# Graph attention on one core: scores with the summed node on the partitions, a fixed softmax shift, values in two column tiles

## The chip, the cores and the metric

One core of one Trainium2 chip. The metric is the device time of one execution in microseconds (us), the median of the runs shown. TensorE is called PE (PEld is its weight loading), VectorE DVE, ScalarE ACT, GpSimd POOL; SP issues DMAs.

## The reference, cut to what matters

x is [8, 2048, 64], adj a [2048, 2048] table of 0 and 1; all else is fp32. All products here are fp32.

```python
def _gat_layer(h, mask, b):                       # h: [..., N, 64]
    scores = einsum('...nd,...md->...nm', h, h)
    scores = where(mask, scores, -1e16)
    attn = softmax(scores, axis=-1)
    return einsum('...nm,...md->...nd', attn, h) + b
mask = adj + eye(N) > 0
h = einsum('bnc,hdc->bhnd', x, Wh)                # 4 heads
out_h = _gat_layer(h, mask, bh)
z = leaky_relu(concat of the heads, 0.2)
h2 = einsum('bnk,dk->bnd', z, Wo)
z2 = leaky_relu(_gat_layer(h2, mask, bo), 0.2)
out = layernorm(x + layernorm(z2) * gamma + beta)
```

The raw scores h h^T are symmetric, and so is nothing else: the mask isn't, and the softmax is taken over m, the summed node.

## The kernel before, in words

Feature maps go in pairs of 64 channels on the 128 partitions (two heads of one batch element in layer 1, two batch elements in layer 2). There are 20 such pairs, called units: 16 of the first layer and 4 of the second. A unit holds hT [128 = 2 x 64 channels, 2048 nodes], which is both operands of the scores, and hN [128 nodes, 16 blocks, A | 1 | B], the values with 64 columns of ones between the two maps.

A unit goes through its 2048 rows n in 8 groups of 256, so there are 160 groups. For a group:

- `scores` (L186): n stands on the partitions, m on the free axis. Map j uses the array's rows 64j to 64j+63, as its 64 channels lie on these partitions. One DVE pass (L192) takes a score tile of 128 x 1024 out of PSUM, adds the mask (0 or -1e16, bf16) and keeps the row's extreme; a small second instruction reads that accumulator. When a row is whole, ACT makes exp with the row's extreme as its bias (L197, 128 x 2048).
- `values` (L210, L213/L215, L226): the product with the values sums over m, so e must have m on the partitions. For each of 16 blocks of m, four 128 x 128 transposes on PE (L210) write one PSUM bank, ACT or DVE copies it out (L215, L213), and two products with hN (L226) take 256 moving columns each. The ones in hN make the denominators come out of the same products, spread over 64 partitions.
- Then DVE takes reciprocals of the denominators (L235, L236), multiplies, adds the bias, applies leaky ReLU (L237 to L241), and `project` (L249, L251) or, in layer 2, `finish` (the LayerNorms, L268 to L293) follows.

The scores of the next group are put between the products of the running one (`between`, called four times). The order on each engine is the scheduler's. POOL has little to do: at the start it turns 16 rows of adj into the mask (L136), and later one small power in each LayerNorm (L283).

A fp32 product shows in the trace as two MATMUL rows, each with its weight load; one such row is called a pass here. A transpose is one pass.

Of the kernel before, what the change touches and what calls it, by code (L numbers as in the profile page):

```python
"""GAT layer (4 heads, then one output layer) over a dense masked graph, leaky ReLU, LayerNorm,
residual, LayerNorm, on one core.

Feature maps are handled in pairs of 64 channels on the 128 partitions: two heads of one batch
element in the first layer, two batch elements in the second. For a pair the kernel holds
  hT [128 = 2 x 64 channels, N]      both operands of the scores
  hN [128 nodes, N / 128, A | 1 | B] the values; the ones give the softmax denominators, already
                                     spread over 64 partitions, in the product that weighs the values.
Rows go through in groups of 256: scores in fp32, the mask added as 0 / -1e16 and the row extreme
taken in one VectorE pass out of PSUM, exp on ScalarE, transposes and values on TensorE. The scores  # L10
of a group are issued between the products of the group before it.
"""
# [1 line left out]

# [6 lines left out]
F32 = mybir.dt.float32  # L21
I32 = mybir.dt.int32
BF16 = mybir.dt.bfloat16
AF = mybir.ActivationFunctionType
OP = mybir.AluOpType
AX = mybir.AxisListType

NEG = -1e16
EPS = 1e-5
SLOPE = 0.2  # L30
FMAX = 3.4028234663852886e38


@with_exitstack
def gat_kernel(ctx: ExitStack, tc: tile.TileContext, x, adj, Wh, bh, Wo, bo, gamma, beta, out):
    nc = tc.nc
    B, N, C = x.shape
    H, D, _ = Wh.shape
    P = 128
    NB = N // P          # blocks of 128 nodes  # L40
    GI = 2               # blocks in a group
    GR = GI * P
    NG = NB // GI
    HP = H // 2
# [7 lines left out]
    psum = ctx.enter_context(tc.tile_pool(name="psum", bufs=2, space=bass.MemoryType.PSUM))  # L52

    def slot(dtype, name):
        """One of the slots of N words that the scores and everything that is only passing share."""
        return epool.tile([P, N], dtype, tag="e", name=name)

    def bank(name):
# [2 lines left out]
    turn = [0]  # L61

    def evacuate(dst, src):
        """PSUM to SBUF, shared between ScalarE and VectorE."""
        turn[0] += 1
        if turn[0] % 2:
            nc.scalar.copy(dst, src)
        else:
            nc.vector.tensor_copy(dst, src)

# [1 line left out]
    ident = const.tile([P, P], F32, name="ident")  # L72
    make_identity(nc, ident)
    whT = const.tile([P, H * D], F32, name="whT")       # [channel (twice), (h d)]
    woT = const.tile([P, HP, D], F32, name="woT")       # [k in a pair of heads, pair, d]
    bh2 = const.tile([P, HP], F32, name="bh2")
    bo2 = const.tile([P, 1], F32, name="bo2")
    gam = const.tile([P, D], F32, name="gam")
# [45 lines left out]
    for t in hNs + [h2N]:  # L124
        nc.gpsimd.memset(t[:, :, 1, :], 1.0)

# [1 line left out]
    bias = {}  # L128

    def load_mask(r):  # L130
# [4 lines left out]
        bias[r] = const.tile([P, N], BF16, name=f"bias{r}")  # L135
        nc.gpsimd.tensor_scalar(bias[r], st, 0.0, NEG, OP.is_le, OP.mult)  # L136

# [1 line left out]
    class Unit:  # L139
        def __init__(self, n, bp, b2, hp):  # L140
            self.n, self.bp, self.b2, self.hp = n, bp, b2, hp
# [26 lines left out]
                    evacuate(self.hN[:, 4 * c:4 * c + 4, 2 * j, :], pv[:, :, j, :])  # L168

        def scores(self, g, step):  # L170
            """Half of the score rows of one block, for both maps; exp once a row is whole."""
            n = self.n
            i, half = divmod(step, 2)
            r = g * GI + i
            if half == 0:
                if r not in bias:
                    load_mask(r)
                for j in range(2):
                    self.E[g, i, j] = (slot(F32, f"e{n}_{g}_{i}_{j}"),
                                       small.tile([P, 2], F32, tag="mx", name=f"mx{n}_{g}_{i}_{j}"))  # L180
            ps = [psum.tile([P, HALF], F32, tag="s", name=f"s{n}_{g}_{step}_{j}") for j in range(2)]
            for c in range(HALF // 512):
                for j in range(2):
                    rows = slice(j * D, (j + 1) * D)
                    c0 = half * HALF + c * 512
                    nc.tensor.matmul(ps[j][:, c * 512:(c + 1) * 512], self.hT[rows, r * P:(r + 1) * P],  # L186
                                     self.hT[rows, c0:c0 + 512], start=True, stop=True)
            cols = slice(half * HALF, (half + 1) * HALF)
            for j in range(2):
                e, mx = self.E[g, i, j]  # L190
                # e = -(scores + bias); mx = its least so far, minus the row's maximum in the end
                nc.vector.tensor_tensor_reduce(  # L192
                    out=e[:, cols], in0=ps[j], in1=bias[r][:, cols], scale=-1.0,
                    scalar=mx[:, 0:1] if half else FMAX, op0=OP.add, op1=OP.min,
                    accum_out=mx[:, half:half + 1])
                if half:
                    nc.scalar.activation(e, e, AF.Exp, bias=mx[:, 1:2], scale=-1.0)  # L197

        def values(self, g, between):
            """The products with the values of a group, `between` called four times on the way.  # L200
            Returns what is left to do with their result."""
            n = self.n
            O = [psum.tile([P, GR], F32, tag=f"o{j}", name=f"o{n}_{g}_{j}", bufs=1) for j in range(2)]

            def turned(m):
                p = bank(f"pt{n}_{g}_{m}")
                for j in range(2):
                    for i in range(GI):
                        k = (j * GI + i) * P
                        nc.tensor.transpose(p[:, k:k + P], self.E[g, i, j][0][:, m * P:(m + 1) * P], ident)  # L210
                t = work.tile([P, 512], F32, tag="et", name=f"et{n}_{g}_{m}", bufs=2)
                if m % 8 in (1, 4, 7):
                    nc.vector.tensor_copy(t, p)  # L213
                else:
                    nc.scalar.copy(t, p)  # L215
                return t

            t = None
            for m in range(NB):
                if m % 4 == 0:  # L220
                    between(m // 4)
                if t is None:
                    t = turned(m)
                ahead = turned(m + 1) if m + 1 < NB else None
                for j in range(2):
                    nc.tensor.matmul(O[j], self.hN[:, m, j:j + 2, :].rearrange("p a d -> p (a d)"),  # L226
                                     t[:, j * GR:(j + 1) * GR], start=(m == 0), stop=(m == NB - 1))
                t = ahead
            for i in range(GI):
                for j in range(2):  # L230
                    del self.E[g, i, j]
            lo, hi = slice(0, D), slice(D, 2 * D)
            rz = work.tile([P, GR], F32, tag="rz", name=f"rz{n}_{g}")
            z = work.tile([P, GR], F32, tag="z", name=f"z{n}_{g}")
            nc.vector.reciprocal(rz[lo], O[0][hi])  # L235
            nc.vector.reciprocal(rz[hi], O[1][lo])  # L236
            nc.vector.tensor_mul(z[lo], O[0][lo], rz[lo])  # L237
            nc.vector.tensor_mul(z[hi], O[1][hi], rz[hi])
            b = bo2 if self.second else bh2[:, self.hp:self.hp + 1]
            nc.vector.tensor_scalar(z, z, b, None, OP.add)  # L240
            nc.vector.scalar_tensor_tensor(z, z, SLOPE, z, OP.mult, OP.max)  # L241
            return lambda: self.finish(g, z) if self.second else self.project(g, z)

        def project(self, g, z):
            """These heads' part of the second layer's feature maps, for the group's nodes."""
            p = bank(f"pp{self.n}_{g}")
            w = woT[:, self.hp, :]
            rows = slice(self.b2 * D, (self.b2 + 1) * D)
# [12 lines left out]
                nc.vector.tensor_add(hN, hN, pn)  # L261

        def finish(self, g, z):
            """LayerNorm, residual and LayerNorm of the group's nodes, in rows."""
            n, K = self.n, 2 * GI
            p = bank(f"pf{n}_{g}")
            for i in range(GI):
# [34 lines left out]
        units.append(Unit(len(units), bp, 0, None))  # L302

    todo = [(u, g) for u in units for g in range(NG)]
    started = False      # whether the scores of this group went out between the last one's products
    rest = None          # what is left of the last group
    xst = None
    for k, (u, g) in enumerate(todo):
        if not started:
            # The second layer needs every node of the first.  # L310
            if rest is not None:
                rest()
                rest = None
            if g == 0:
                u.prepare()
            for s in range(2 * GI):
                u.scores(g, s)
# [19 lines left out]
    rest()  # L337


# [1 line left out]
_INS = ["x", "adj", "L0_gnn_Wh", "L0_gnn_bh", "L0_gnn_Wo", "L0_gnn_bo", "L0_gnn_gamma", "L0_gnn_beta"]  # L341
_OUTS = [((8, 2048, 64), "float32")]
# [23 lines left out]
```

## Time and profile before

| | |
|---|---|
| Median of 3 runs | 6328.17 us (6324.19 to 6332.58) |
| Span of the profiled execution, first to last instruction | 6325.3 us |
| Busy shares of the span | PE 96%, PEld 60%, DVE 53%, ACT 34%, POOL 3% |
| Mean granted PE clock, as a share of 2.4 GHz | 0.981 |
| DMA over the span | 29.60 MB, mean 5 GB/s |

The span is the profiled execution's own time from its first to its last instruction. The median of the runs lies 2.9 us over it; that is what stands around it, launch and end, and chance. A timeline row gives start, duration, engine, line, operation, tiles, form and count of instructions merged. For PE the durations overlap: a MATMUL's row lasts beyond the start of the next, so what a pass takes in a stream is the distance from start to start.

### The profile page before, as it was taken

How to read it: one execution, taken by the hardware profiler on the slowest of the kernel's cores; microseconds unless marked ns; L12 is line 12 of the kernel's file. 1: busy time of each engine (PE TensorE's matmuls, PEld its weight loads, DVE VectorE, ACT ScalarE, POOL GpSimd, SP SyncE). 2: the span in 40 equal slices, each digit the busy share in tenths (PEclk: the TensorE clock that was granted, in tenths of full speed). 3: DMA queues.
4: the chain of work that ended last, by engine and by line, in shares of the span. 5: the costliest groups of instructions: out<-in, count | busy, mean ns of one | idle time of the engine just before them, and what ended most of it. 6: DMA issues, size and time to landing. Idle time of an engine off the chain costs nothing.

```text
span 6325.3 us, 65156 instructions
## 1 busy us (share of the span) xinstructions
PE 6055.8 (96%) x27204; PEld 3770.4 (60%) x27204; DVE 3348.6 (53%) x5402; ACT 2170.2 (34%) x2345; POOL 184.6 (3%) x95
## 2 busy tenths in 40 slices
PE   7899999999999999999999999999999999999998
PEld 4556666655566666665556666566555666666555
DVE  4445555556555555555655555555565555555555
ACT  2233333333333333333333333333333333333332
POOL 3210000000000000000000000000000000000000
PEclk9899999999999999999999999999999999999999
DMA  1100000000000000000000000000000000000000
GB/s 62 40 14 1 1 1 1 1 1 11 3 1 1 1 1 1 1 1 1 11 3 1 1 1 1 1 1 1 9 4 2 1 1 1 1 1 1 1 3 5
DMA packets 37303, 29.60 MB, mean 5 GB/s; under 512 B 34864, under 2 KB 34928, under 8 KB 34960
## 3 DMA queue, kind: packets, MB, share of 16 engines
q1 hardware_dynamic: 36224, 25.17, 1.4%
q8 instruction: 213, 3.49, 0.2%
q14 instruction: 82, 0.67, 0.0%
q10 hardware_dynamic: 624, 0.20, 0.0%
q0 software_dynamic: 160, 0.07, 0.0%
HBM read 21.24 MB, written 4.19 MB: 4 GB/s over the span
## 4 chain that ended last, share of the span: by engine, by line
PE 76%; ACT 12%; DVE 7%; POOL 2%; issue 2%; DMA 1%; ACTq 0%; POOLq 0%; SPq 0%; DVEq 0%
PE o L226 30%; PE s L186 26%; PE pt L210 16%; ACT e L197 9%; ACT et L215 2%; DVE e L192 2%; POOL bias L136 1%; PE pp L251 1%; PE pp L249 1%; POOL st L283 1%; PE pn L164 1%; PE ph L157 1%; DVE et L213 1%; DMA adj<-in_adj_dram 0%; DVE st L281 0%
## 5 line engine op out<-in xcount | busy, mean ns | idle before, releaser
L226 PE MATMUL o<-et,hN 128*128 128x256 f32 x8192 | 2160.0, 389 | 110.1 <-ACT et L215 84.3
L215 ACT COPY et<-pt 128x512 f32<-128x512 f32 x1600 | 931.4, 583 | 3677.4 <-PE pt L210 3190.2
L186 PE MATMUL s<-hT 64*128 64x512 f32 x4096 | 1766.0, 640 | 34.3 <-DVE mx L192 34.3
L226 PEld LDWEIGHTS o<-et,hN 128*128 128x128 f32 x8192 | 1422.9, 192 | 606.0 <-ACT et L215 280.3
L210 PEld LDWEIGHTS pt<-ident,e 128*128 128x128 f32 x10240 | 1211.0, 142 | 822.1 <-ACT et L215 256.0
L210 PE MATMUL pt<-ident,e 128*128 128x128 f32 x10240 | 1596.5, 279 | 25.2 <-DVE y L289 11.5
L213 DVE COPY et<-pt 128x512 f32<-128x512 f32 x960 | 661.5, 689 | 1463.7 <-PE pt L210 973.1
L197 ACT ACTIVATE e<-e,mx 128x2048 f32<-128x2048 f32 x640 | 1262.7, 2001 | 263.8 <-DVE mx L192 252.3
L192 DVE CUSTOM_DVE_ANT_0 e<-s,bias 128x1024 f32<-128x1024 f32 x640 | 772.0, 1223 | 732.0 <-PE s L186 634.0
L192 DVE CUSTOM_DVE_ANT_0 e<-s,bias,mx 128x1024 f32<-128x1024 f32 x640 | 806.5, 1281 | 394.4 <-PE s L186 394.4
L186 PEld LDWEIGHTS s<-hT 64*128 64x128 f32 x4096 | 529.6, 188 | 536.7 <-issue 450.6
L226 PE MATMUL o<-et,h2N 128*128 128x256 f32 x2048 | 545.5, 392 | 39.9 <-ACT et L215 21.9
L186 PE MATMUL s<-h2T 64*128 64x512 f32 x1024 | 453.8, 660 | 28.3 <-DVE mx L192 28.3
L226 PEld LDWEIGHTS o<-et,h2N 128*128 128x128 f32 x2048 | 357.2, 194 | 147.9 <-ACT et L215 52.6
L235 DVE RECIPROCAL rz<-o 64x256 f32<-64x256 f32 x160 | 281.4, 1759 | 191.3 <-PE o L226 191.2
L236 DVE RECIPROCAL rz<-o 64x256 f32<-64x256 f32 x160 | 280.1, 1751 | 5.1
L186 PEld LDWEIGHTS s<-h2T 64*128 64x128 f32 x1024 | 137.6, 193 | 172.0 <-issue 110.0
L283 POOL TENSOR_TENSOR st<-st,mhalf 128x4 f32<-128x4 f32 x64 | 64.5, 1007 | 5889.0 <-DVE st L282 5889.0
L136 POOL TENSOR_SCALAR bias<-adj 128x2048 bf16<-128x2048 int32 x16 | 113.6, 7097 | 246.9 <-DVE adj L134 246.9
L192 DVE DVE_READ_ACCUMULATOR2_ANT mx<- 128x1 f32 x1280 | 106.2, 83 | 0.0
L251 PEld LDWEIGHTS pp<-woT,z 128*128 128x128 f32 x512 | 69.6, 197 | 52.8 <-issue 52.8
L241 DVE SCALAR_TENSOR_TENSOR z<-z 128x256 f32<-128x256 f32 x160 | 88.0, 550 | 0.2
(60 smaller groups left out, 1100.1 us busy)
## 6 DMA issues: line engine op xcount, KB each, us to landing
adj<-in_adj_dram SPq DMA_DIRECT2D x16, 1024.0 KB, 6.8
x<-in_x_dram SPq DMA_DIRECT2D x8, 512.0 KB, 5.6
out_dram<-y SPq DMA_DIRECT2D x64, 64.0 KB, 1.7
ws<-in_L_gnn_Wh_dram ACTq DMA_DIRECT2D x2, 64.0 KB, 4.4
ws<-in_L_gnn_Wo_dram ACTq DMA_DIRECT2D x1, 64.0 KB, 4.6
bo<-in_L_gnn_bo_dram POOLq DMA_DIRECT2D x2, 0.2 KB, 5.5
gam<-in_L_gnn_gamma_dram POOLq DMA_DIRECT2D x1, 32.0 KB, 5.6
bet<-in_L_gnn_beta_dram POOLq DMA_DIRECT2D x1, 32.0 KB, 5.2
```

The costliest lines, as they stand in the source:

```text
L136: nc.gpsimd.tensor_scalar(bias[r], st, 0.0, NEG, OP.is_le, OP.mult)
L186: nc.tensor.matmul(ps[j][:, c * 512:(c + 1) * 512], self.hT[rows, r * P:(r + 1) * P], self.hT[rows, c0:c0 + 512], start=True, stop=True)
L192: nc.vector.tensor_tensor_reduce(out=e[:, cols], in0=ps[j], in1=bias[r][:, cols], scale=-1.0, scalar=mx[:, 0:1] if half else FMAX, op0=OP. ...
L197: nc.scalar.activation(e, e, AF.Exp, bias=mx[:, 1:2], scale=-1.0)
L210: nc.tensor.transpose(p[:, k:k + P], self.E[g, i, j][0][:, m * P:(m + 1) * P], ident)
L213: nc.vector.tensor_copy(t, p)
L215: nc.scalar.copy(t, p)
L226: nc.tensor.matmul(O[j], self.hN[:, m, j:j + 2, :].rearrange("p a d -> p (a d)"), t[:, j * GR:(j + 1) * GR], start=(m == 0), stop=(m == NB ...
L235: nc.vector.reciprocal(rz[lo], O[0][hi])
L236: nc.vector.reciprocal(rz[hi], O[1][lo])
L251: nc.tensor.matmul(p[:, GR + i * D:GR + (i + 1) * D], z[:, i * P:(i + 1) * P], w, start=True, stop=True)
L283: nc.gpsimd.tensor_tensor(st[:, 3, :], st[:, 2, :], mhalf, OP.pow)
```

## The change

The kernel becomes two programs behind each other. `fast_kernel` is new; `general_kernel` is the kernel before, unchanged, and runs only if a flag says so. The order on each engine in the new program is the order in which it is written (`manual_schedule`).

In `fast_kernel` the summed node m is on the partitions. Work goes in **periods**: 4 blocks m of 128 nodes against a chunk c of 512 rows n, for both maps of a unit. 4 periods make a chunk, 16 a unit, 320 all. In a period:

- `scores`: for each m, two products (map 0 on the array's rows 0 to 63, map 1 on 64 to 127) give 128 x 1024; DVE subtracts the mask (0 or 1e16, bf16, now stored transposed, one tile read for both maps); ACT takes exp with one constant shift per layer (78, and 62 in layer 2) in place of the row's extreme. A score tile takes two PSUM banks, and there are three of them.
- `values`: for each m of the period before, map j's 64 value columns are the weights, exp of map j is moving (512 columns), and the result goes to partitions 64j to 64j+63 of one bank. So each product uses 64 of the array's 128 columns. No transposes of e, no copies of them, no ones.
- `add_up`: the denominators. POOL adds three of four exp tiles (128 x 1024) into `acc`, DVE adds the fourth into `accd`.
- After a chunk, spread over the six next periods: `finish0` (ACT copies the result out of PSUM, DVE adds accd to acc), `finish1` (a product with ones sums acc over the partitions), `finish2` (the sums go by DMA to 128 partitions x 8, reciprocal, by DMA through DRAM and back, spread over 64 partitions), `finish3` (multiply, leaky ReLU), `finish4` (projection, or in layer 2 transposes and the first LayerNorm), `finish5` (layer 2: the rest).
- The biases are added to the values (bhb, bob), since the weights of a row sum to 1. hN is made by transposes of hT. The mask's 32 half rows are turned by PE transposes (bf16) at the start and during the first periods. Layer 2 of a pair of batch elements runs after the first unit of the next pair (the last two at the end), so that it need not wait for the projections of its own first layer.
- At the end the sums of all denominators and of their reciprocals on each partition are compared with e^83 and e^63, and a flag goes to DRAM. If one is over its limit, `general_kernel` computes everything again.

```diff
+        def scores(self, c, m):
+            ps = spsum(f"s{self.n}_{c}_{m}")
+            for j in range(2):
+                rows = slice(j * D, (j + 1) * D)
+                nc.tensor.matmul(ps[:, j * W:(j + 1) * W], self.hT[rows, m * P:(m + 1) * P],
+                                 self.hT[rows, c * W:(c + 1) * W], start=True, stop=True)
+            e = slot([P, 2, W], F32, f"e{self.n}_{c}_{m}")
+            nc.vector.tensor_tensor(e, ps.rearrange("p (j i) -> p j i", j=2),
+                                    mask[c][:, m, :].unsqueeze(1).to_broadcast([P, 2, W]), OP.subtract)
+            nc.scalar.activation(e, e, AF.Exp, bias=shifts[:, 1:2] if self.second else shifts[:, 0:1], scale=1.0)
+            return e
+
+        def values(self, c, m, e):
+            if m == 0:
+                self.O[c] = psum.tile([P, W], F32, tag="o", name=f"o{self.n}_{c}", bufs=1)
+            for j in range(2):
+                nc.tensor.matmul(self.O[c][j * D:(j + 1) * D, :], self.hN[:, m, j * D:(j + 1) * D], e[:, j, :],
+                                 start=(m == 0), stop=(m == NB - 1))
+
+        def add_up(self, c, es):
...
+            for e in es[:3]:
+                nc.gpsimd.tensor_tensor(self.acc[c], self.acc[c], e, OP.add)
...
+                nc.vector.tensor_tensor(t, t, es[3], OP.add)
...
+        def finish0(self, c):
+            self.osb[c] = wtile(f"osb{self.n}_{c}")
+            nc.scalar.copy(self.osb[c], self.O[c])
+            nc.vector.tensor_tensor(self.acc[c], self.acc[c], self.accd[c][0], OP.add)
+
+        def finish1(self, c):
...
+            for j in range(2):
+                nc.tensor.matmul(pz[j * D:(j + 1) * D, :], ones, self.acc[c][:, j, :], start=True, stop=True)
...
+        def finish3(self, c):
+            z = self.osb[c]
+            nc.vector.tensor_tensor(z, z, self.rz[c], OP.mult)
+            nc.vector.scalar_tensor_tensor(z, z, SLOPE, z, OP.mult, OP.max)
...
+    for t in range(total + 1):
+        now = []
+        if t < total:
+            u, c, q = periods[t]
+            now = [u.scores(c, q * BATCH + k) for k in range(BATCH)]
+        if t > 0:
+            u, c, q = periods[t - 1]
+            for k in range(BATCH):
+                u.values(c, q * BATCH + k, es[k])
+            u.add_up(c, es)
+        es = now
+        for job in jobs.pop(t, ()):
+            job()
...
+    nc.vector.tensor_scalar(fl, pf[0:1, 0:1], P - 0.5, None, OP.is_lt)
+    nc.sync.dma_start(out=flag, in_=fl)
+
+
+def gat_kernel(tc: tile.TileContext, x, adj, Wh, bh, Wo, bo, gamma, beta, out):
+    nc = tc.nc
+    with tc.tile_pool(name="flags", bufs=1, space=bass.MemoryType.DRAM) as pool:
+        flag = pool.tile([1, 1], I32, name="flag")
+        with tc.manual_schedule():
+            fast_kernel(tc, x, adj, Wh, bh, Wo, bo, gamma, beta, out, flag)
+        again = nc.values_load(flag, min_val=0, max_val=1)
+        with tc.If(again > 0):
+            general_kernel(tc, x, adj, Wh, bh, Wo, bo, gamma, beta, out)
```

On PE before, the middle of a group of the first layer. s are scores, pt transposes of e, et their copies, o the products with the values; the last numbers of a name tell tiles apart.

```order
L210 MATMUL pt_2_1_5744<-ident,e_2_1_0_5628 128x128
L210 MATMUL pt_2_1_5744<-ident,e_2_0_1_5523 128x128
L210 MATMUL pt_2_1_5744<-ident,e_2_1_1_5630 128x128
L186 MATMUL s_3_1_0_5780<-hT_5070 128x512
L210 MATMUL pt_2_2_5753<-ident,e_2_0_0_5521 128x128
L210 MATMUL pt_2_2_5753<-ident,e_2_1_0_5628 128x128
L210 MATMUL pt_2_2_5753<-ident,e_2_0_1_5523 128x128
L210 MATMUL pt_2_2_5753<-ident,e_2_1_1_5630 128x128
L186 MATMUL s_3_1_0_5780<-hT_5070 128x512
L226 MATMUL o_2_0_5723<-et_2_0_5742,hN_106 128x256
L226 MATMUL o_2_1_5724<-et_2_0_5742,hN_106 128x256
```

On PE in the new program, one period of the first layer (each x2 is map 0, then map 1), with the sum over the partitions of the chunk before (pz) behind it:

```order
L520 MATMUL s_0_4_5763<-hT_5437 128x512 x2
L520 MATMUL s_0_5_5769<-hT_5437 128x512 x2
L520 MATMUL s_0_6_5775<-hT_5437 128x512 x2
L520 MATMUL s_0_7_5781<-hT_5437 128x512 x2
L532 MATMUL o_0_5787<-e_0_0_5724,hN_5530 64x512 x2
L532 MATMUL o_0_5787<-e_0_1_5730,hN_5530 64x512 x2
L532 MATMUL o_0_5787<-e_0_2_5736,hN_5530 64x512 x2
L532 MATMUL o_0_5787<-e_0_3_5742,hN_5530 64x512 x2
L566 MATMUL pz_3_5799<-acc_3_5626,ones 64x512 x2
```

The transposes and the copies that they waited for have left the stream, and scores and values alternate in blocks of eight products, the values one period behind.

On DVE in the new program, a period that ends a chunk and the one after it. e are the subtractions of the mask, accd and acc the sums for the denominators, osb the result of the chunk before:

```order
L523 TENSOR_TENSOR e_3_15_10107<-s_3_15_10104,mask_124 128x1024
L553 TENSOR_TENSOR accd_3_10075<-accd_3_10075,e_3_11_10061 128x1024
L589 TENSOR_TENSOR osb_2_9993<-osb_2_9993,rz_2_10083 128x512
L590 SCALAR_TENSOR_TENSOR osb_2_9993<-osb_2_9993 128x512
L523 TENSOR_TENSOR e_0_0_10127<-s_0_0_10124,mask_121 128x1024
L523 TENSOR_TENSOR e_0_1_10133<-s_0_1_10130,mask_121 128x1024
L523 TENSOR_TENSOR e_0_2_10139<-s_0_2_10136,mask_121 128x1024
L523 TENSOR_TENSOR e_0_3_10145<-s_0_3_10142,mask_121 128x1024
L553 TENSOR_TENSOR accd_3_10075<-accd_3_10075,e_3_15_10107 128x1024
L560 TENSOR_TENSOR acc_3_10029<-acc_3_10029,accd_3_10075 128x1024
```

Every period's four subtractions stand in one block, and what a chunk leaves to do stands between two blocks, ahead of the next period's first subtraction.

## Rows read from the trace of the kernel before

**Rows 1.** The page: span, busy time by engine, granted clock in 40 slices.

```profile
span 6325.3 us, 65156 instructions
PE 6055.8 (96%) x27204; PEld 3770.4 (60%) x27204; DVE 3348.6 (53%) x5402; ACT 2170.2 (34%) x2345; POOL 184.6 (3%) x95
PEclk9899999999999999999999999999999999999999
```

**Rows 2.** Groups by line, busy us, mean ns, idle us before and its releasers.

```profile
L226 PE MATMUL o<-et,hN 128*128 128x256 f32 x8192 | 2160.0, 389 | 110.1 <-ACT et L215 84.3 <-DVE et L213 22.1 <-DVE z L237 3.7
L186 PE MATMUL s<-hT 64*128 64x512 f32 x4096 | 1766.0, 640 | 34.3 <-DVE mx L192 34.3
L210 PE MATMUL pt<-ident,e 128*128 128x128 f32 x10240 | 1596.5, 279 | 25.2 <-DVE y L289 11.5 <-ACT et L215 6.3 <-DVE xT L69 4.7
L210 PEld LDWEIGHTS pt<-ident,e 128*128 128x128 f32 x10240 | 1211.0, 142 | 822.1 <-ACT et L215 256.0 <-PE s L186 191.0 <-issue 158.8
```

**Rows 3.** Timeline of the last group, PE and PEld, where no scores are left.

```profile
6300.19 0.60 PE L210 MATMUL pt<-ident,e 128*128 128x128 f32 x4
...
6300.62 1.03 PE L226 MATMUL o<-et,h2N 128*128 128x256 f32 x4
...
6301.49 0.60 PE L210 MATMUL pt<-ident,e 128*128 128x128 f32 x4
```

**Rows 4.** Timeline, PE: scores of one row tile alone, then what follows them.

```profile
2004.02 1.12 PE L186 MATMUL s<-hT 64*128 64x512 f32 x2
2005.07 1.13 PE L226 MATMUL o<-et,hN 128*128 128x256 f32 x4
...
2007.43 1.98 PE L186 MATMUL s<-hT 64*128 64x512 f32 x6
2009.34 0.66 PE L210 MATMUL pt<-ident,e 128*128 128x128 f32 x4
```

**Rows 5.** Timeline, PE: scores of both row tiles, then what follows them.

```profile
3001.71 1.13 PE L186 MATMUL s<-h2T 64*128 64x512 f32 x4
3002.77 0.66 PE L210 MATMUL pt<-ident,e 128*128 128x128 f32 x4
```

**Rows 6.** Timeline, DVE: two score tiles on each other's heels, and 256 columns.

```profile
2999.99 0.41 DVE L289 TENSOR_TENSOR y<-y,pf 128x256 f32<-128x256 f32 x1
3000.43 0.42 DVE L277 TENSOR_REDUCE st<-y 128x4 f32<-128x256 f32 x1
...
3004.15 1.22 DVE L192 CUSTOM_DVE_ANT_0 e<-s,bias 128x1024 f32<-128x1024 f32 x1
3005.30 1.22 DVE L192 CUSTOM_DVE_ANT_0 e<-s,bias 128x1024 f32<-128x1024 f32 x1
```

**Rows 7.** Groups by line, DVE and ACT, columns as in Rows 2.

```profile
L197 ACT ACTIVATE e<-e,mx 128x2048 f32<-128x2048 f32 x640 | 1262.7, 2001 | 263.8 <-DVE mx L192 252.3 <-PE o L226 10.6
L215 ACT COPY et<-pt 128x512 f32<-128x512 f32 x1600 | 931.4, 583 | 3677.4 <-PE pt L210 3190.2 <-PE o L226 486.6 <-DVE y L284 0.7
L213 DVE COPY et<-pt 128x512 f32<-128x512 f32 x960 | 661.5, 689 | 1463.7 <-PE pt L210 973.1 <-ACT e L197 483.2 <-issue 7.1
L241 DVE SCALAR_TENSOR_TENSOR z<-z 128x256 f32<-128x256 f32 x160 | 88.0, 550 | 0.2
```

**Rows 8.** Groups by line, POOL.

```profile
L136 POOL TENSOR_SCALAR bias<-adj 128x2048 bf16<-128x2048 int32 x16 | 113.6, 7097 | 246.9 <-DVE adj L134 246.9
L283 POOL TENSOR_TENSOR st<-st,mhalf 128x4 f32<-128x4 f32 x64 | 64.5, 1007 | 5889.0 <-DVE st L282 5889.0
L125 POOL MEMSET hN<- 128x1024 f32 x2 | 1.9, 970 | 0.0
```

**Rows 9.** DMA issues: KB each, median us from issue to landing.

```profile
adj<-in_adj_dram SPq DMA_DIRECT2D x16, 1024.0 KB, 6.8
x<-in_x_dram SPq DMA_DIRECT2D x8, 512.0 KB, 5.6
out_dram<-y SPq DMA_DIRECT2D x64, 64.0 KB, 1.7
```

More of the change, by code (lines that the diff above doesn't have):

```diff
@@ L13 @@
 from contextlib import ExitStack
+import math
 import concourse.bass as bass
@@ L31, with general_kernel @@
 FMAX = 3.4028234663852886e38
+BIG = 1e16
+SHIFT1 = 78.0
+SHIFT2 = 62.0
+LOG_TOP = 83.0
+LOG_LOW = -63.0
 @with_exitstack
-def gat_kernel(ctx: ExitStack, tc: tile.TileContext, x, adj, Wh, bh, Wo, bo, gamma, beta, out):
+def general_kernel(ctx: ExitStack, tc: tile.TileContext, x, adj, Wh, bh, Wo, bo, gamma, beta, out):
     nc = tc.nc
@@ new lines, in gat_kernel @@
+def gat_kernel(tc: tile.TileContext, x, adj, Wh, bh, Wo, bo, gamma, beta, out):
+    nc = tc.nc
+    with tc.tile_pool(name="flags", bufs=1, space=bass.MemoryType.DRAM) as pool:
[5 more added lines that the diff above has]
+            general_kernel(tc, x, adj, Wh, bh, Wo, bo, gamma, beta, out)
```

293 lines of the change are left out of this document (added).

## Prediction

> **What bounds the kernel now.** I read the page first: PE is busy 96% of the span, no other engine over 60%, and the granted clock is full in nearly every slice [rows 1]. So time is saved only where PE has less to do or waits less. The groups by line say what PE does: 10240 transposes, and 10240 passes of values (8192 of them in the row shown) against 5120 passes of scores (4096 in theirs) [rows 2]. Their mean durations overlap, so what they cost is read from starts in the timeline. At the very end, where no scores are left, four transposes take 0.43 us and four value passes of 256 columns 0.87 us, so that a block of m costs 1.30 us [rows 3]. That makes 0.109 us per transpose and 0.435 us per 512 columns of a pass; a group has 16 blocks, and 160 groups x 16 x 1.30 us = 3330 us, over half of the span. Next, the scores: two passes take 1.05 us from start to the next line's start, which is 2 x 0.43 + 0.19; I take 0.19 as the price of changing from one kind of tile to another. Six passes take 1.91 us, that is 4 x 0.43 + 0.19, not 6 [rows 4]; four take 1.06 us [rows 5]. So passes on the two halves of the array's rows run side by side, and a pair costs one slot of 0.43 us. Last, the weight loads of the transposes sat idle for 822 us, mostly behind copies and other tiles [rows 2]: besides its work PE waits for the copies of the transposes that it made.
>
> **What the change takes away.** The transposes, 10240 x 0.109 = 1116 us, with the waits for their copies. Of the values, half: before, a pass had 128 weight columns, 64 of them ones for the denominators; now two products with 64 columns each could stand side by side. The reciprocals of 64 x 256 tiles go too, from DVE.
>
> **PE's new stream.** A period has 16 passes of scores on two row tiles, so 8 slots: 8 x 0.43 + 0.19 = 3.63 us [rows 4, 5]. It has 16 passes of values on two column tiles. No stretch of the trace has two column tiles at work, so this is bounded: side by side like row tiles, 8 slots, 3.63 us; one behind the other, 16 slots, 7.07 us. I take side by side, as the row tiles are the nearest thing seen, and keep the other end as a rival. A period is then 7.26 us, and 320 of them 2323 us. Beside them, for a unit of layer 1: hT, 8 passes on one row tile in two parts, 2 x (4 x 0.43 + 0.19) = 3.8 us; 16 transposes for hN, 1.7 + 2 x 0.19 = 2.1; for each of four chunks the sum over partitions and the projection, 2 slots each, 2 x 1.05 = 2.1, so 8.4. Together 14.3 x 16 units = 229 us. For layer 2: 2.1 and per chunk 1.05 + 4 transposes 0.6, so 8.7 x 4 = 35. Turning x: 64 x 0.109 = 7. Sum of PE: 2594 us.
>
> **The other engines.** DVE: two score tiles on each other's heels start 1.15 us apart, and 256 columns take 0.44 [rows 6]; I take 1.15 for 1024 columns, 0.69 for 512 [rows 7], 0.9 for the leaky ReLU of 512 (0.55 for 256, [rows 7]). Layer 1, per chunk: 16 subtractions 18.4, four sums 4.6, normalising 1.6, half a projection add 0.35, small ones 0.5, hN 0.6: 26 us, against PE's 4 x 7.26 + 3.6 = 32.6. So DVE has time, but its order is fixed. The first scores of a period are ready 1.05 us after it begins; four subtractions end at 5.65; the next period's first scores come at 8.3. With three score buffers, the first subtraction may be some 0.6 us late before PE stands, so 2.65 + 0.6 = 3.25 us of other work fits between two blocks. A chunk's end leaves 1.15 + 1.15 in one gap and 1.15 + 1.6 in another: both fit, just. ACT: exp of 1024 is between the copy of 512, 0.58, and the exp of 2048, 2.0 [rows 7]; by the line through them 1.06, four are 4.2 us, far below a period.
>
> POOL is the unknown. Per period it makes 2.75 sums of 128 x 1024 in fp32, and the trace has none. Below, a memset of that size took 0.97 us, writing only; above, half of the mask's 7.10 us for 2048, that is 3.55, reading one stream of another type with two operations [rows 8]. A sum moves three streams: 2.9 us if they took turns, 1.9 if writing hides. I take 2.4, near the middle: 6.6 us a period, under 7.26. The Trainium skill (GPSIMD Engine Reference, 3.1) gives 4497 ns for a sum of 2048, by estimate 2.25 us for 1024, and 6.2 us a period; it holds POOL the wrong engine for such sums, and no run here shows it yet.
>
> A sum on POOL and a DVE instruction with both inputs in SBUF may also stand in each other's way: the trace has nothing to tell. From below it costs nothing; from above each of DVE's two lumps per chunk waits out one POOL sum of 2.4 us. I take 0.9 us beyond the gap, twice in each of 64 chunks: 115 us. (The Trainium skill, SBUF — State Buffer, Who interferes with whom, says the two share a read port as an exclusive lock, held for the whole instruction, which speaks for the upper end, 307 us instead of 115.)
>
> Layer 2 has larger lumps. A LayerNorm step on 512 columns is four passes of 0.69, two small ones of 0.17, a square on ACT of 0.6 and the power on POOL, 1.0 [rows 7, 8], with hops 5.1 us. One gap then holds 1.15 + 1.15 + 5.1 = 7.4, the next 1.15 + 3 x 0.69 + 5.1 = 8.3, against 3.25: 4.1 + 5.1, with the waits on POOL some 10 us a chunk, x 16 = 160 us.
>
> Ends. Before the first scores, x and 4 MB of adj must land: 6.8 us a MB [rows 9], about 36 us, and the last half row be turned and hT made, 45 in all. The other 24 half rows cost DVE and ACT about 1.3 us each over what hides, 30. At the end the chain of sums, three DMAs of about 2 us (1.7, [rows 9]), two LayerNorm steps and the flag: 40.
>
> **The sum.** 2594 + 115 + 160 + 45 + 30 + 40 = 2984, to be set against the span of 6325.3; with the 3 us around a span, and not more exact than tens, **2980 us**.
>
> **Rivals.**
>
> *Column tiles one behind the other.* For it: two moving streams then need all 128 partitions each, which no row here shows. Against it: row tiles do run abreast [rows 5], with 64 partitions each. Values take 3.44 us more a period, 1101 us, and the sums over partitions 64 x 0.86 + 16 x 0.86 = 69; DVE's lumps (275 us) then fit. 2980 + 1170 - 275 = about 3870 us.
>
> *POOL decides.* At 3.55 us a sum, a period needs 9.8 us, and as exp tiles come free only when POOL is done, everything follows it: 320 x 9.8 + 85 = 3220; if DVE's two-input work (1.6 us a period) shuts it out besides, 3730. In the middle 3470. The point is 7.26 / 2.75 = 2.64 us a sum.
>
> *The flag is set, and both programs run.* Then 2980 + 6325 = 9300 us, slower than before. It decides when, on some partition, the denominators reach e^83 or their reciprocals e^63. From the reference's inputs, the logarithm of a denominator lies between -57.7 and 78.7 in layer 1 (shift 78) and -45.8 and 65.7 in layer 2 (shift 62); all of them summed make 79.3, and the reciprocals 58.7, so even the whole sum would pass. What is left is arithmetic on the chip that differs in large measure.
>
> **How the numbers follow.** Forecast 0.70, column tiles in turn 0.13, POOL 0.15, flag 0.02. The forecast's own bounds: without any lumps and with a shorter start 2594 + 60 = about 2650; with the upper ends, 307 for the lumps and half as much again for layer 2 and the ends, 3300. The range reaches on into POOL's case up to 3650; left out are the column tiles in turn, the flag and some 4 in 100 around. Three cases are faster; a measurement of this kernel can tell 0.2%, some 13 us, from no change. Faster 0.975, within 0.2% 0.005, slower 0.02.
>
> **What would show it.** Right: no L210 to L226 rows run; value rows (L532) come in pairs whose starts lie a few ns apart, eight slots in about 3.6 us; PE near 90% with a clock near 0.98; DVE and POOL each 75 to 95%. The POOL sum's mean is the first number to read: over 2.64 us makes POOL the bound. Value passes 0.43 us apart without overlap mean the second rival. Wrong in another way: score passes waiting for DVE in every period rather than around chunk ends and in layer 2, or a clock at 1.2 GHz in stretches where PE waits.

## The result and the profile after

The changed kernel takes 3554.94 us (median of 4, 3553.44 to 3559.79) against 6327.82 before: a ratio of 0.5619, with a 95% interval of 0.5611 to 0.5627. That is faster, as forecast, and inside the range, but 575 us over the 2980 that was said. The profiled execution has a span of 3551.6 us.

The page of the changed kernel, the lines that answer to [rows 1]:

```profile
span 3551.6 us, 31313 instructions
PE 2870.1 (81%) x11526; PEld 986.6 (28%) x11526; DVE 2963.9 (83%) x2368; ACT 1654.9 (47%) x1577; POOL 2363.0 (67%) x929
PEclk8779999999988899999998899999999999988886
```

No engine is full: PE, which was to be the bound, works 81% of the span. Its groups by line, and DVE's and POOL's costliest (columns as in [rows 2]):

```profile
L545 POOL TENSOR_TENSOR acc<-acc,e 128x1024 f32<-128x1024 f32 x720 | 1869.8, 2597 | 467.2 <-ACT e L525 421.1
...
L523 DVE TENSOR_TENSOR e<-s,mask 128x1024 f32<-128x1024 f32 x1280 | 1477.6, 1212 | 278.5 <-PE s L520 266.6 <-remote 11.1
L520 PE MATMUL s<-hT 64*128 64x512 f32 x4096 | 1096.5, 646 | 340.5 <-DVE e L523 284.5 <-DVE hN L513 55.9
L532 PE MATMUL o<-e,hN 128*64 128x512 f32 x5120 | 1285.2, 648 | 0.0
...
L553 DVE TENSOR_TENSOR accd<-accd,e 128x1024 f32<-128x1024 f32 x160 | 310.4, 1940 | 0.0
...
L589 DVE TENSOR_TENSOR osb<-osb,rz 128x512 f32<-128x512 f32 x80 | 220.1, 2751 | 4.9 <-DMA rz<-rd 4.9
L590 DVE SCALAR_TENSOR_TENSOR osb<-osb 128x512 f32<-128x512 f32 x80 | 210.8, 2635 | 2.8
...
L560 DVE TENSOR_TENSOR acc<-acc,accd 128x1024 f32<-128x1024 f32 x80 | 169.4, 2118 | 2.8
L579 DVE TENSOR_TENSOR stat<-stat,zt 128x8 f32<-128x8 f32 x80 | 169.3, 2116 | 0.0
```

Read the means. The mask's subtraction takes 1.21 us, as [rows 6] had it. But the multiply of 512 columns (L589) takes 2.75 us where such a pass cost 0.69 [rows 7], the leaky ReLU (L590) 2.64, and a sum of *eight* columns (L579) 2.12. These have two inputs in SBUF; the subtraction has one there and one in PSUM. PE's scores of layer 1 wait 284.5 us for DVE.

Two pieces of PE's timeline show that both kinds of tiles run abreast, 16 passes of 512 columns each:

```profile
61.92 3.65 PE L532 MATMUL o<-e,hN 128*64 128x512 f32 x16
...
470.18 3.70 PE L520 MATMUL s<-hT 64*128 64x512 f32 x16
473.82 2.37 PE L532 MATMUL o<-e,hN 128*64 128x512 f32 x10
```

A chunk of layer 1 on DVE in the changed kernel; a period runs from one block of four subtractions to the next:

```profile
453.15 4.60 DVE L523 TENSOR_TENSOR e<-s,mask 128x1024 f32<-128x1024 f32 x4
457.68 2.52 DVE L553 TENSOR_TENSOR accd<-accd,e 128x1024 f32<-128x1024 f32 x1
461.67 0.68 DVE L604 TENSOR_TENSOR h2T<-h2T,pp 64x512 f32<-64x512 f32 x1 [1.47 <-PE pp L599]
462.27 1.22 DVE L560 TENSOR_TENSOR acc<-acc,accd 128x1024 f32<-128x1024 f32 x1
463.42 4.60 DVE L523 TENSOR_TENSOR e<-s,mask 128x1024 f32<-128x1024 f32 x4
471.36 4.62 DVE L523 TENSOR_TENSOR e<-s,mask 128x1024 f32<-128x1024 f32 x4 [3.34 <-PE s L520]
475.90 1.54 DVE L549 TENSOR_TENSOR accd<-e,e 128x1024 f32<-128x1024 f32 x1
...
477.47 2.20 DVE L579 TENSOR_TENSOR stat<-stat,zt 128x8 f32<-128x8 f32 x1
479.60 0.15 DVE L580 TENSOR_TENSOR stat<-stat,rt 128x8 f32<-128x8 f32 x1
479.67 4.60 DVE L523 TENSOR_TENSOR e<-s,mask 128x1024 f32<-128x1024 f32 x4
484.20 1.48 DVE L553 TENSOR_TENSOR accd<-accd,e 128x1024 f32<-128x1024 f32 x1
485.60 2.83 DVE L589 TENSOR_TENSOR osb<-osb,rz 128x512 f32<-128x512 f32 x1
488.47 2.71 DVE L590 SCALAR_TENSOR_TENSOR osb<-osb 128x512 f32<-128x512 f32 x1
491.10 2.34 DVE L523 TENSOR_TENSOR e<-s,mask 128x1024 f32<-128x1024 f32 x2
```

The four periods are 10.27, 7.94, 8.31 and 11.43 us, 37.95 a chunk; 7.26 was the bound by PE, without what a chunk's end adds there. The stretched instructions stand in the other three periods, and in these DVE is at work nearly all the time between two blocks (in the first it also waits 1.47 us for PE's projection, L599). Where no instruction was stretched (7.94), DVE waited 3.34 us for PE, as it should.

What the stretched ones wait out is seen in a piece of layer 2, DVE's and POOL's timelines of the changed kernel:

```profile
1010.11 2.33 POOL L541 TENSOR_TENSOR acc<-e,e 128x1024 f32<-128x1024 f32 x1
1012.52 2.67 POOL L542 TENSOR_TENSOR acc<-acc,e 128x1024 f32<-128x1024 f32 x1
```

```profile
1010.16 2.83 DVE L642 TENSOR_TENSOR y<-y,st 128x512 f32<-128x512 f32 x1 [1.78 <-POOL st L641]
1012.92 3.35 DVE L560 TENSOR_TENSOR acc<-acc,accd 128x1024 f32<-128x1024 f32 x1
```

POOL starts a sum at 1010.11, DVE its multiply 0.05 us later; POOL ends at 1012.44, DVE at 1012.99, 0.55 us behind it. Then POOL's next sum and DVE's next do the same: DVE ends at 1016.27, 1.08 us behind POOL. The whole trace says the same. Of the 80 multiplies (L589), 77 began while POOL was at a sum, and each ended 0.55 us behind that sum, within 0.01; the other three began with POOL idle and took 0.69. The sum of eight columns (L579) ended 0.02 us behind POOL's sum 77 times, and took 0.12 us the three times that POOL was idle.

### The profile page after: what moved, and what is told of

It reads as the page before. It is cut to its first block, busy times and chain, and to the rows that moved or that the text cites. A ratio compares the mean times of both kernels' runs of the same rounds, so it can differ in the third digit from the quotient of the medians.

```text
span 3551.6 us, 31313 instructions
## 1 busy us (share of the span) xinstructions
PE 2870.1 (81%) x11526; PEld 986.6 (28%) x11526; DVE 2963.9 (83%) x2368; ACT 1654.9 (47%) x1577; POOL 2363.0 (67%) x929
## 4 chain that ended last, share of the span: by engine, by line
PE 38%; DVE 29%; issue 19%; POOL 8%; DMA 4%; ACT 2%; SPq 0%; DVEq 0%; POOLq 0%; ACTq 0%
PE o L532 17%; PE s L520 15%; DVE e L523 11%; POOL acc L545 5%; DVE osb L589 5%; DVE accd L553 4%; DMA rz<-rd 4%; DVE acc L560 3%; PE ph L501 2%; PE pz L566 2%; POOL acc L542 1%; DVE y L642 1%; POOL acc L541 1%; ACT e L525 1%; PE pp L599 1%
## 5 line engine op out<-in xcount | busy, mean ns | idle before, releaser
L545 POOL TENSOR_TENSOR acc<-acc,e 128x1024 f32<-128x1024 f32 x720 | 1869.8, 2597 | 467.2 <-ACT e L525 421.1
L525 ACT ACTIVATE e<-e,shifts 128x1024 f32<-128x1024 f32 x1280 | 1451.0, 1149 | 1355.6 <-DVE e L523 1348.3
L523 DVE TENSOR_TENSOR e<-s,mask 128x1024 f32<-128x1024 f32 x1280 | 1477.6, 1212 | 278.5 <-PE s L520 266.6
L520 PE MATMUL s<-hT 64*128 64x512 f32 x4096 | 1096.5, 646 | 340.5 <-DVE e L523 284.5
L532 PE MATMUL o<-e,hN 128*64 128x512 f32 x5120 | 1285.2, 648 | 0.0
L532 PEld LDWEIGHTS o<-e,hN 128*64 128x64 f32 x5120 | 367.1, 149 | 933.8 <-issue 712.5
L541 POOL TENSOR_TENSOR acc<-e,e 128x1024 f32<-128x1024 f32 x80 | 188.9, 2362 | 345.6 <-ACT e L525 345.6
L553 DVE TENSOR_TENSOR accd<-accd,e 128x1024 f32<-128x1024 f32 x160 | 310.4, 1940 | 0.0
L542 POOL TENSOR_TENSOR acc<-acc,e 128x1024 f32<-128x1024 f32 x80 | 248.6, 3107 | 6.3
L589 DVE TENSOR_TENSOR osb<-osb,rz 128x512 f32<-128x512 f32 x80 | 220.1, 2751 | 4.9 <-DMA rz<-rd 4.9
L590 DVE SCALAR_TENSOR_TENSOR osb<-osb 128x512 f32<-128x512 f32 x80 | 210.8, 2635 | 2.8
L579 DVE TENSOR_TENSOR stat<-stat,zt 128x8 f32<-128x8 f32 x80 | 169.3, 2116 | 0.0
L642 DVE TENSOR_TENSOR y<-y,st 128x512 f32<-128x512 f32 x32 | 81.8, 2555 | 56.3 <-POOL st L641 56.3
```

The source lines that it names most:

```text
L520: nc.tensor.matmul(ps[:, j * W:(j + 1) * W], self.hT[rows, m * P:(m + 1) * P], self.hT[rows, c * W:(c + 1) * W], start=True, stop=True)
L523: nc.vector.tensor_tensor(e, ps.rearrange("p (j i) -> p j i", j=2), mask[c][:, m, :].unsqueeze(1).to_broadcast([P, 2, W]), OP.subtract)
L525: nc.scalar.activation(e, e, AF.Exp, bias=shifts[:, 1:2] if self.second else shifts[:, 0:1], scale=1.0)
L532: nc.tensor.matmul(self.O[c][j * D:(j + 1) * D, :], self.hN[:, m, j * D:(j + 1) * D], e[:, j, :], start=(m == 0), stop=(m == NB - 1))
L541: nc.gpsimd.tensor_tensor(self.acc[c], es[0], es[1], OP.add)
L542: nc.gpsimd.tensor_tensor(self.acc[c], self.acc[c], es[2], OP.add)
```

## The experiments

Each time below is of one execution, but where a ratio stands beside it the median of four. Theory 1: a DVE instruction with two SBUF inputs and a POOL instruction that reads SBUF shut each other out, and each such DVE instruction waits anew. Theory 2: the chunk ends hold PE up by their number and place in DVE's order. Theory 3: POOL's length sets the pace.

**POOL writes, and reads nothing.** DVE's and PE's orders are kept.

```diff
-            for e in es[:3]:
-                nc.gpsimd.tensor_tensor(self.acc[c], self.acc[c], e, OP.add)
+            for _ in range(8):
+                nc.gpsimd.memset(self.acc[c], 1.0)
```

> POOL's sums are replaced by memsets that write the accumulator and read nothing: eight of about 0.97 us in place of three sums (7.8 us for 7.8), six in place of two. The denominators then leave out three of four exp tiles, and the shift of layer 1 is 160 so that the numbers stay finite. DVE's and PE's orders are as in the changed kernel. Theory 1 (the shared port: a DVE instruction with two SBUF inputs and a POOL instruction that reads SBUF shut each other out): accd sums fall from 1.94 to 1.2 us, the multiply and the leaky ReLU from 2.7 to 0.7, the small stat sum from 2.1 to 0.15; a chunk of layer 1 goes from 37.9 to 32 us and the time from 3555 to about 3050. Theory 2 (the chunk ends hold up PE by their number and their place in DVE's order, whatever POOL does): durations as they are, time over 3450. Theory 3 (POOL's length sets the pace): POOL is as long as before, so over 3450 as well.

Measured: 2889.17 us, span 2886.5. The same chunk in DVE's timeline of this kernel:

```profile
373.62 4.62 DVE L523 TENSOR_TENSOR e<-s,mask 128x1024 f32<-128x1024 f32 x4
378.15 1.22 DVE L553 TENSOR_TENSOR accd<-accd,e 128x1024 f32<-128x1024 f32 x1
...
382.36 4.60 DVE L523 TENSOR_TENSOR e<-s,mask 128x1024 f32<-128x1024 f32 x4
390.30 4.62 DVE L523 TENSOR_TENSOR e<-s,mask 128x1024 f32<-128x1024 f32 x4 [3.34 <-PE s L520]
...
396.08 0.12 DVE L579 TENSOR_TENSOR stat<-stat,zt 128x8 f32<-128x8 f32 x1
...
397.52 4.62 DVE L523 TENSOR_TENSOR e<-s,mask 128x1024 f32<-128x1024 f32 x4 [1.15 <-PE s L520]
402.06 1.21 DVE L553 TENSOR_TENSOR accd<-accd,e 128x1024 f32<-128x1024 f32 x1
403.19 0.69 DVE L589 TENSOR_TENSOR osb<-osb,rz 128x512 f32<-128x512 f32 x1
403.91 0.69 DVE L590 SCALAR_TENSOR_TENSOR osb<-osb 128x512 f32<-128x512 f32 x1
404.74 2.36 DVE L523 TENSOR_TENSOR e<-s,mask 128x1024 f32<-128x1024 f32 x2
```

```profile
PE 2658.3 (92%) x11526; PEld 958.9 (33%) x11526; DVE 2204.1 (76%) x2368; ACT 1652.4 (57%) x1577; POOL 2340.6 (81%) x2449
```

POOL is as busy as before (2340.6 us against 2363.0), DVE has the same 2368 instructions and is 760 us less busy, PE is at 92%, and the periods of this chunk are 8.74, 7.94, 7.22 and 7.22 us, 31.12 in all: 7.2 where a chunk's end adds nothing to PE's stream. That settles it against theories 2 and 3: 665 us of the changed kernel's span come from POOL's reading. A memset also waits for no exp tile and holds none, which a sum does; but in the changed kernel's trace no engine's idle time ended with a POOL sum (of what POOL makes, only the small power was waited for, 56.3 us, and the identity at the start, 1.3), so that isn't the cause. In size theory 1 fell short too; it expected 3050.

**POOL copies, with one input.** The same with three copies and one memset a period:

```diff
+            for e in es[:3]:
+                nc.gpsimd.tensor_copy(self.acc[c], e)
+            nc.gpsimd.memset(self.acc[c], 1.0)
```

> As e1_pool_writes_only, but POOL copies three exp tiles a period into the accumulator (two for a chunk's first period) and then sets it: it reads SBUF with one input instead of two. The denominators leave out three of four tiles. If any reading on POOL shuts DVE's two-input instructions out, the multiply and the leaky ReLU take up to a copy's length more than 0.69 us; a copy of 1024 columns should take 1 to 2.3 us, so 1.5 to 2.5 us each, and a time between 2950 and 3400. If only POOL instructions with two inputs do, 0.69 us and about 2890.

Measured: 2982.52 us. The multiply took 1.49 us, the sum of eight columns 0.85; the leaky ReLU behind the multiply 0.69. DVE's groups by line:

```profile
L591 DVE TENSOR_TENSOR osb<-osb,rz 128x512 f32<-128x512 f32 x80 | 119.0, 1487 | 5.0 <-DMA rz<-rd 5.0
```

So one input read on POOL is enough to shut DVE out. The wait is shorter, as a copy is (1.23 us in the mean) and as POOL was less busy. That the leaky ReLU didn't wait wasn't expected, but the timelines of POOL and DVE tell why:

```profile
415.33 0.95 POOL L547 MEMSET acc<- 128x1024 f32 x1
415.84 0.69 DVE L592 SCALAR_TENSOR_TENSOR osb<-osb 128x512 f32<-128x512 f32 x1
```

The multiply ahead of it had waited out POOL's last copy, so it met the memset, 77 times in 80; the other three times POOL was idle.

**All sums on DVE.**

```diff
-            for e in es[:3]:
-                nc.gpsimd.tensor_tensor(self.acc[c], self.acc[c], e, OP.add)
...
+            for e in es:
+                nc.vector.tensor_tensor(self.acc[c], self.acc[c], e, OP.add)
...
-            nc.vector.tensor_tensor(self.acc[c], self.acc[c], self.accd[c][0], OP.add)
```

> All sums of exp tiles go to DVE, 15 a chunk; POOL is left with the small powers. Theory 1: each sum takes 1.2 us and no two-input instruction is stretched, so a chunk of layer 1 costs DVE 16 x 1.13 + 15 x 1.13 + about 3 = 38 us, the same as the 37.9 now: 3500 to 3700, although DVE does 11 sums more a chunk. Theory 2: a sum takes 1.94 us as now by itself, so a chunk costs 18 + 15 x 1.94 + 8 = 55 us: over 4500.

Measured: 3601.84 us. The chunk's first sum took 1.215 us in the mean, the multiply 0.69. With POOL idle but for the small powers, the kernel took 47 us (1.3%) more than with POOL taking 11 of 15 sums, too little in one execution to build on: about what POOL's help saved on DVE it cost there.

**The chunk's end off the port.** The leaky ReLU before the multiply with one input in PSUM, the multiply on POOL, acc and accd summed on PE, the flag's sums in columns of their own:

```diff
-            nc.vector.tensor_tensor(self.acc[c], self.acc[c], self.accd[c][0], OP.add)
+            nc.vector.scalar_tensor_tensor(self.osb[c], self.osb[c], SLOPE, self.O[c], OP.mult, OP.max)
...
+                nc.tensor.matmul(pz[j * D:(j + 1) * D, :], ones, self.accd[c][0][:, j, :], start=False, stop=True)
...
-            nc.vector.tensor_tensor(z, z, self.rz[c], OP.mult)
-            nc.vector.scalar_tensor_tensor(z, z, SLOPE, z, OP.mult, OP.max)
+            nc.gpsimd.tensor_tensor(z, z, self.rz[c], OP.mult)
```

> What a chunk leaves to do loses its DVE instructions with two SBUF inputs: the leaky ReLU is taken before the multiply (it commutes with a positive factor) with one input still in PSUM, the multiply goes to POOL, acc and accd are both summed over the partitions on PE instead of added first, and the sums for the flag go to columns of their own. The accd sums (three a chunk) stay. Theory 1: no leaky ReLU over 0.8 us; the periods of a layer 1 chunk go from 10.3, 7.9, 8.3, 11.4 to about 8.3, 7.9, 7.9, 8.3; 80 x 5.5 = 440 us less, so about 3120; POOL's sums keep about 2.5 us. Theory 2 (number of instructions): DVE loses 4 of 9 chunk-end instructions with nominal 1.15 + 0.7 + 0.3 us, 80 x 2.1 = 170 less at most, about 3390.

Measured: 3066.99 us. The leaky ReLU took 0.68 us (2.64 in the changed kernel), and from the second period on the blocks of this kernel's chunk start 8.91, 7.22 and 7.22 us apart:

```profile
439.43 4.60 DVE L522 TENSOR_TENSOR e<-s,mask 128x1024 f32<-128x1024 f32 x4
448.34 4.62 DVE L522 TENSOR_TENSOR e<-s,mask 128x1024 f32<-128x1024 f32 x4 [4.32 <-PE s L519]
...
455.56 4.62 DVE L522 TENSOR_TENSOR e<-s,mask 128x1024 f32<-128x1024 f32 x4 [1.09 <-PE s L519]
...
462.78 2.36 DVE L522 TENSOR_TENSOR e<-s,mask 128x1024 f32<-128x1024 f32 x2 [0.80 <-PE s L519]
```

These three blocks wait for PE's scores (4.32, 1.09 and 0.80 us), so PE bounds three of the four periods now; the 8.91 hold the longer sum on PE. The gain is 488 us where four instructions of nominally 2.1 us a chunk would have given 170.

**Layer 2's LayerNorms spread.** Six jobs, one a period, in place of two; same instructions, same engines.

```diff
-                for d, f in enumerate((u.finish0, u.finish1, u.finish2, u.finish3, u.finish4, u.finish5)):
+                for d, f in enumerate((u.finish0, u.finish1, u.finish2, u.finish3, u.finish4,
+                                       u.finish5, u.finish6, u.finish7, u.finish8, u.finish9)):
```

> Only layer 2's LayerNorms change: the two steps are cut into six jobs, one per period, instead of two, with the same instructions on the same engines. If the long periods of layer 2 (20 and 14 us against 10 and 8) come from DVE waiting within a job for ACT's square and POOL's power, then 16 chunks x about 12 us go: about 3370. If they come from the two-input instructions alone (multiplies by the scale, gamma, the sum of beta and x), these are now met by POOL's sums in every period and cost 2.5 us each instead of 0.7: 3500 to 3600.

Measured: 3478.06 us, between the two: 77 us gained. The periods of 20 and 14 us fell to 14 and 10, but the other two of such a chunk rose from 8 and 11 to 15 and 13.

**Both, with layer 2's products on POOL.** As the last two together, scale, gamma, beta and x by `nc.gpsimd`.

> The kernel of e3_chunk_end_off_port, and layer 2's LayerNorms cut into six jobs as in e4_norm_spread, with their two-input products and sums (scale, gamma, beta, x) on POOL instead of DVE. Layer 2 held some 27 us a chunk-pair over layer 1 in e3 (periods of 15 and 14.5 against 8.6 and 8.9). Theory 1: with DVE left no two-input instruction there, these fall to about 9 and 9.5: 16 chunks x 11 us = 180 us less than 3067, about 2890; POOL gains 5 x 1.3 us a chunk, for which it has room. Theory 2 (number and order): the same, so no test between the two; a third way, POOL's queue making the LayerNorm late for the next chunk, would show as periods of over 10 us and a time over 3000.

Measured: 3051.41 us, 16 (0.5%) less than without, not 180: the third way. In its timelines POOL adds x behind three sums, and DVE stands for the mean:

```profile
970.48 8.09 POOL L545 TENSOR_TENSOR acc<-acc,e 128x1024 f32<-128x1024 f32 x3
978.53 1.26 POOL L631 TENSOR_TENSOR y<-y,xr 128x512 f32<-128x512 f32 x1
```

```profile
979.82 0.69 DVE L653 TENSOR_REDUCE st<-y 128x8 f32<-128x512 f32 x1 [5.87 <-POOL y L631]
```

**The mask in two steps.** In addition, a half row is made on ACT in one period and turned on PE in the next. All half rows go to ACT then, where DVE had made half of them, and in another order.

```diff
+        at(t, job)
+        at(t + 1, lambda k=k: mask_turn(*halves[k - AHEAD], turns.pop(k)))
```

> The kernel of e5_norm_on_pool, and the mask's half rows made in two steps: the row on ACT in one period, its turning on PE and the copy on DVE in the next, so that PE does not stand in front of a row that is being made; the DVE instruction that made half of the rows (2.8 us beside POOL's sums, 0.68 alone) is gone. The first unit took 245 us against 133 for a plain one. If PE's place behind the row was the cause, some 60 to 80 us go, about 2810; if the loads of adj are, under 20 go.

Measured: 2941.09 us, ratio to before 0.4648 (0.4639 to 0.4656); 110 us gained. What it removes, in the changed kernel's timeline:

```profile
96.29 2.83 DVE L460 TENSOR_SCALAR mrow<-adj 128x1024 bf16<-128x1024 int32 x1
...
99.17 0.62 PE L463 MATMUL pm<-identb,mrow 128*128 128x128 bf16 x8 [3.98 <-DVE mrow L460]
```

PE's next scores stood behind this transpose; the row that it waited for was made late and, beside POOL's sums, in 2.83 us for 0.68. The idle time of PE before these transposes fell from 88.0 us to 8.7, first without the split, then with it:

```profile
L462 PE MATMUL pm<-identb,mrow 128*128 128x128 bf16 x256 | 29.5, 286 | 88.0 <-DVE mrow L459 50.2 <-ACT mrow L457 37.7
L462 PE MATMUL pm<-identb,mrow 128*128 128x128 bf16 x256 | 20.8, 241 | 8.7 <-ACT mrow L456 8.6
```

So PE's place behind the rows was the cause, and worth more than the 60 to 80 us expected: the first unit went from 245.0 to 146.2 us, and its first subtraction began 11.7 us earlier. How much is due to the split and how much to the rows' leaving DVE, the run doesn't part.

**x a job early.** In addition, POOL adds x right behind beta.

> The kernel of e6_mask_split; in layer 2, x is loaded a job earlier and POOL adds it right behind beta, a period before DVE needs the sum, not in the same job in which DVE takes the mean of it. In e5 and e6 every fourth period of layer 2 took 16 us against 7.2, with DVE idle for 5.9 us before that mean, behind POOL's three sums and the sum of x. If that wait makes the period long, it falls to 10 or 11 us (the subtraction of the mean still has two SBUF inputs, 2.5 us beside POOL), 16 chunks x 5 us = 80 us less than 2941: about 2860. If POOL is simply full there, the wait moves to the next job and nothing is gained: 2920 to 2950.

Measured: 2902.61 us, ratio 0.4582 (0.4574 to 0.459): 38 us gained, half of what was expected; the 16 us period fell to 8.7, but another rose from 8.9 to 10.8. This is the best version run, 18% under the changed kernel.

**The flag set.** Limit e^10 for e^83.

> The changed kernel with the limit for the denominators at e^10 instead of e^83, so the flag is set for these inputs and the exact program runs behind the first. All theories: 3555 + 6325 and some 10 us for starting it, about 9890, which prices the rival in which both programs run.

Measured: 9876.38 us, 6 us less than the changed kernel and the kernel before together (9882.8). So the rival in which both programs run is priced by adding their times; the 9300 that it was given fell short only as the first program did.

## Why the prediction was right or wrong

*The direction, and PE's new stream: right.* Column tiles run abreast: 3.65 us for 16 passes, said 3.63. The period came out at 7.2 us wherever nothing held PE, said 7.26. Take the 115 us for the two engines in each other's way out of the sum, and 2869 us are left; with POOL's reading gone the span is 2886.5. That the other terms together come within 1% is luck in part. By the starts of the subtractions in that trace, the first one began at 53.6 us, said 45, and the first unit took 190.6 us against 129.4 for the second, 61 for the mask's rows where 30 was said; so the rest of the terms together was some 22 us too high.

*The step that failed:* "I take 0.9 us beyond the gap, twice in each of 64 chunks: 115 us." Measured, POOL's reading costs 665 us over the whole kernel. In the chunk of layer 1 shown it is 37.95 - 31.12 = 6.83 us, about 437 us for 64 chunks where 115 was said; the rest lies mostly in layer 2 and in the first unit (247.7 us against 190.6), for which the term had nothing. Two things were wrong in it. It counted one wait for a lump, while L589 and L590, one behind the other, each wait out a sum of their own (2.83 and 2.71 us): the two periods with a lump grew by 1.53 and 4.21 us, not by 0.9 each. And it counted lumps of long instructions only; the sum of eight columns, put down under "small ones 0.5", takes 2.1 us, and its period, counted as free, grew by 1.09. Even the upper end, 307 us, was for one wait a lump. The sentence of the Trainium skill (SBUF — State Buffer, Who interferes with whom) that the shared read port is an exclusive lock held for the whole instruction agrees with the trace: DVE ends a little less than its own length behind POOL's sum (0.55 us of 0.69, and 1.08 of 1.21), and a memset, which only writes, delays none of the two-input instructions. As a rule it was stated in the prediction, and priced too low.

*POOL as the bound: wrong, and near.* A sum takes 2.34 to 2.40 us where none of these DVE instructions overlaps it (2.4 was taken) and 2.60 in the mean, as it waits for DVE too; 2.64 was the point. But POOL waited 421 us for ACT before these sums, and the run in which it wrote for as long was fast: it wasn't its length.

*Lumps that fit:* right without the lock, as the prediction said, "just". With POOL writing only, 1.15 + 1.4 us between two blocks left the period at 7.22 us. Behind 1.15 + 1.15 and the wait for the projection, PE's scores stood 0.27 us.

*The start:* 45 us to the first scores; the first subtraction began at 48.9. "30" for the mask's other half rows was too low: it priced the work and not PE's standing. The run that split their making gained 110 us, start included, and 79 of that is PE's idle time before the transposes.

*The clock* was granted at 0.91 over the span, and at 0.966 with POOL writing only; 0.98 was said. It follows PE's standing: from 466 to 471 us, with PE busy throughout, it was at the upper of its two levels, 2.4 GHz (1.00); from 1000 to 1040 us, with PE busy for 28 of 40 us, it was 0.81 in the mean. The same 11526 passes kept PE busy for 2870.1 us against 2658.3, so some of the 665 us may come by way of the clock; no run parts that from the waits.

## What to carry to other kernels

Giving work to POOL isn't free for DVE: while POOL reads SBUF, a DVE instruction with two SBUF inputs waits for the end of POOL's instruction, however small it is, and the next one waits again if POOL has begun its next by then. (The second sum of eight columns, L580, right behind the first, took 0.15 us.) Count such instructions, not their columns; make them read PSUM with one input, give them to POOL itself or to PE's accumulation, and leave on DVE what reads one SBUF tensor, after a look at its row in the trace (the next section has a form that waits all the same). In an order written by hand, put what makes an operand a period ahead of what waits for it, on PE above all.

## What was not expected of the hardware

A sum of 128 x 8 on DVE took 2.12 us in the mean beside POOL's sums and 0.12 without them. POOL's own sums were stretched less, 2.60 in the mean for 2.34 to 2.40, and a copy on POOL, reading one tensor, blocked DVE as well. A DVE instruction with a scalar operand and one input (the mask's row, 0.68 us alone) was stretched to 2.83 beside them, so two SBUF inputs aren't the only form that is shut out. POOL's writing alone stretched this one: in the run with memsets it took 1.00 us in the mean and up to 1.55, while the two-input instructions kept their 0.12, 0.69 and 1.21 us there.
